# SiLU as one ScalarE instruction in the first scan of a scan-plus-attention kernel

## The chip, the core and the metric

The kernel runs on one core of a Trainium2 chip. The core has five engines that each take their instructions in order from a queue of their own and wait for each other through semaphores: TensorE (PE, with weight loads listed apart as PEld), VectorE (DVE), ScalarE (ACT), GpSimd (POOL) and SyncE (SP), which here only issues DMAs. The metric is the device time of one execution in microseconds (us), as the median of several runs. A lower time is better.

## The reference, cut to what matters

The input `x` has 32 sequences of 256 tokens with 256 channels. Two blocks follow each other: a gated state-space block with a recurrence over time, and two layers of local attention with a feed-forward part. The change touches only the first block:

```python
xr, gate = jnp.split(x @ W_in.T, 2, axis=-1)
xr = xr + t_emb[:, None, :]
xc = depthwise causal convolution of xr with 4 taps, + b_conv
xc = silu(xc)
xn = (xc - mean) / sqrt(var + 1e-5) * ln_g + ln_b
Bm, Cm, dt = split(xn @ W_xproj.T, 3)
dt = tanh(dt @ W_dt.T + b_dt) * 0.01
Ad = 1.0 - dt * tanh(A_log)
Bd = Bm * minimum(norm(xn), 1.0)
h  = clip(h * Ad + Bd * x_t, -10, 10)          # 256 steps, one after the other
y  = einsum(C_t, h) + D * xn
return (y * silu(gate)) @ W_out.T
```

`silu(v) = v * sigmoid(v)`, which is `0.5 * v * (1 + tanh(v / 2))`. The attention layers use `exp`, the feed-forward layers an exact `gelu`.

## The kernel before

**Tiling.** The 32 sequences are done in four groups of eight (`GB = 8`). In each group the recurrence walks through 256 steps in eight chunks of 32 (`CH = 32`); a step works on one tile of 128 partitions (16 states by 8 sequences) by 512 channels. While the attention and feed-forward layers of one group run, mainly on TensorE, the scan of the next group runs beside them. The first group's scan (`alone = g == 0`) has no layers beside it. TensorE uses that stretch to project the inputs of the three later groups ahead of time (`ahead_load`, `ahead_project`, `ahead_copy`, `ahead_put`).

**A chunk of the scan.** `project` multiplies the input by `W_in` into a PSUM bank, 128 channels at a time, so four of the eight projections feed the convolution and four the gate. `conv_in` (L471, L477) adds the condition on VectorE and starts the convolution on GpSimd; `conv_taps` (L488) adds three taps on VectorE. `conv_th` (L496) then puts `tanh(acc / 2)` into a tile `th` on ScalarE, and `conv_out` (L501) makes `(th + 1) * acc` on VectorE, which is twice the SiLU, in the tile `xc`. From `xc` TensorE makes the products `ps_raw` (L510) and the transpose `tp_x` (L540); VectorE takes its mean and variance (L550 to L554), ScalarE normalises (L569), GpSimd applies gain and offset (L576, L577), and SP writes the rows to DRAM as `xnd` (L581). The doubled SiLU changes nothing in the normalised value because the variance gets `4 * LN_EPS` in place of `LN_EPS`.

**A step.** SP loads row `t` of `xnd` into a tile `xrep`, repeated over the 16 states (`load_rows`, L675), from a pool of six buffers; in the first scan two rows in eight are spread by a matmul instead (`spread_rows`, L683). ScalarE scales the row by `beta` (`scale_row`, L696). VectorE then does the step itself, add and clip, as one custom instruction (`step`, L706) that needs the `h` of the step before. TensorE reads the output out of `h` (`read_out`, L718).

**The gate.** `gate_th` copies the gate's projection from PSUM into `sg` in the scan's order of tokens (`reorder`, L371, ScalarE) and puts its `tanh(sg / 2)` into `th_g` (L756, ScalarE). `gate_out` (L761) makes `(th_g + 1) * sg` on VectorE. `out_gate` (L787) multiplies it with the transposed scan output. The factor of two is taken out by `halve`, which multiplies `W_out` by 0.5 once. `project_y` (L796) and `copy_y` (L807) finish the block.

**Order of the work.** `at(slot, what)` writes an agenda by hand: conv work of a chunk 38 to 29 steps ahead of its first step, gate work 15 to 22 steps into the chunk. Tiles and waits come from pools; a scheduler in the recording layer then decides the order in which each engine's instructions stand, so removing an instruction can also move others. An order fixed by `tc.keep_in_program_order` is kept.

**ScalarE's tables.** ScalarE holds one set of activation functions at a time. The loads that change the set stand in the program as ACT_TABLE_LOAD; in the kernel before there is one at the start (L316), and then 123 ahead of `exp` (L1191) and 124 ahead of `gelu` (L1346), all of them after the first scan.

Of the kernel before, what the change touches and what calls it, by code (L numbers as in the profile page):

```python
# [13 lines left out]
AF = mybir.ActivationFunctionType  # L14
# [10 lines left out]
NC_ = DI // P  # L25
# [18 lines left out]
LN_EPS = 1e-5  # L44
# [29 lines left out]
def kernel(  # L74
# [29 lines left out]
    nc = tc.nc  # L104
# [58 lines left out]
    for j in range(NJ):  # L163
# [18 lines left out]
        out=mask_t[:, 0:W], in_=mask_t[:, 0:W], compare_op=ALU.is_ge, fill=MASKED_LOW,  # L182
# [3 lines left out]
        out=mask_t[:, W : 2 * W], in_=mask_t[:, W : 2 * W], compare_op=ALU.is_ge,  # L186
# [30 lines left out]
    for i in range(2):  # L217
        t = const.tile([P, NI * (P + GB)], FP, tag=f"ly{i}", name=f"ly{i}")
# [3 lines left out]
    def program(ctx, exact):  # L222
# [143 lines left out]
            for n in range(2 * L):  # L366
                at(50 + 6 * n, tables, n // L, n % L)

        def reorder(out, ps):

            nc.scalar.copy(  # L371
                out.rearrange("p (q i b) -> p b i q", q=NQ, b=GB),
                ps.rearrange("p (b i q) -> p b i q", q=NQ, b=GB),
            )

        def group_scan(g):
# [8 lines left out]
            alone = g == 0  # L385
# [3 lines left out]
            ck = [{} for _ in range(NCH)]  # L389

            def at(s, what, *args):
                agendas[-1].setdefault(s, []).append(partial(what, *args))
# [99 lines left out]

            def conv_th(c, ch):
                acc = ck[c]["xr", ch][1]
                th = sp.tile([P, GB * CH], FP, tag="th", name="th", bufs=2)
                nc.scalar.activation(th, acc.rearrange("p b t -> p (b t)"), AF.Tanh, scale=0.5)  # L496
                ck[c]["th", ch] = th
# [49 lines left out]
            def norm_stats(c, j):  # L547
                tp, stat = ck[c]["tp", j], ck[c]["stat"]
                st = sm.tile([P, 6], FP, tag="st", name="st")
                nc.vector.bn_stats(st, tp)  # L550
                mv = sm.tile([P, 2], FP, tag="mv", name="mv")
                nc.vector.bn_aggr(mv, st)
                ve = sm.tile([P, 1], FP, tag="ve", name="ve")
                nc.vector.tensor_scalar_add(ve, mv[:, 1:2], 4 * LN_EPS)  # L554
                nc.gpsimd.tensor_tensor(stat[:, j, 0:1], ve, neg_half[:, 0:1], ALU.pow)
                ck[c]["mv", j] = mv

# [192 lines left out]
            def gate_th(c, ch):  # L750
                if ch == 0:
                    ck[c]["sg"] = sp.tile([P, NC_, GB * CH], FP, tag="sg", name="sg")
                sg = ck[c]["sg"][:, ch]
                reorder(sg, ck[c].pop(("ps", NC_ + ch)))
                th = sp.tile([P, GB * CH], FP, tag="th", name="th_g", bufs=2)
                nc.scalar.activation(th, sg, AF.Tanh, scale=0.5)  # L756
                ck[c]["th_g", ch] = th
# [46 lines left out]

            def copy_y(c, d):
                yo = sp.tile([P, GB, CH], FP, tag="yo", name="yo", bufs=2)
                nc.scalar.copy(  # L807
                    yo.rearrange("p b (i q) -> p q i b", q=NQ),
                    ck[c].pop(("po", d))[:, 0 : GB * CH].rearrange(
                        "p (q i b) -> p q i b", q=NQ, b=GB  # L810
                    ),
                )
                ck[c]["yo", d] = yo

# [27 lines left out]
            for c in range(NCH):  # L842
                s0 = c * CH
                for hb in range(CH // TB):
                    s = s0 + hb * TB
                    for i in range(NI):
                        at(s + 4 * i + 5, read_out, c, hb, i)
                    at(s + 21, gated, c, hb)
                    at(s + 25, out_gate, c, hb)
                    at(s + 11, skip, c, hb)  # L850
                for ch in range(NC_):
                    at(s0 - 38 + 2 * ch, conv_in, c, ch)
                    at(s0 - 37 + 2 * ch, conv_taps, c, ch)
                    at(s0 - 36 + 2 * ch, conv_th, c, ch)
                    at(s0 - 35 + 2 * ch, conv_out, c, ch)
                for ch, s in enumerate((13, 16, 17, 18)):
                    at(s0 + s + 2, gate_th, c, ch)
                    at(s0 + s + 4, gate_out, c, ch)
                at(s0 - 25, raw_copy, c)
                at(s0 - 24, raw_turn, c)  # L860
                for j in range(NJ):
                    s = s0 - 26 + 4 * j
                    at(s + 2, norm_stats, c, j)
                    at(s + 4, norm_shift, c, j)
                    at(s + 5, norm_apply, c, j)
                    at(s + 6, norm_affine, c, j)
                    at(s + 9, norm_out, c, j)
                at(s0 - 11, length, c)
                at(s0 - 9, figures, c)
                at(s0 - 7, figures_in, c)  # L870
                at(s0 - 6, decay_th, c)
                at(s0 - 5, decays, c)
                at(s0 - 4, put_c, c, 0)
                at(s0 + 4, put_c, c, 1)
                for d in range(KM):
                    at(s0 + 45 + 2 * d, copy_y, c, d)
                    at(s0 + 46 + 2 * d, put_y, c, d)
            agendas.append({})
            for c in range(NCH):
                s0 = c * CH  # L880
# [19 lines left out]
                for hb in range(CH // TB):  # L900
                    s = s0 + hb * TB
# [5 lines left out]
            if alone:  # L907
                n = (NG - 1) * NCH * 2
                for u in range(n):
                    s = -30 + u * (NCH * CH) // n  # L910
# [6 lines left out]
        def scan_slots(groups):  # L917


            slots, scans = {}, [group_scan(g) for g in groups]  # L920
            for part in range(2):
                for i, agendas in enumerate(scans):
                    for s, what in agendas[part].items():
                        slots.setdefault(i * S + s, []).extend(what)
            for s in range(min(slots), max(slots) + 1):
                for what in slots.get(s, ()):
                    what()
                yield s
# [104 lines left out]
        if exact:  # L1033
# [4 lines left out]
                out=mask[:, 0:W], in_=mask[:, 0:W], compare_op=ALU.is_ge, fill=MASKED,  # L1038
# [3 lines left out]
                out=mask[:, W : 2 * W], in_=mask[:, W : 2 * W], compare_op=ALU.is_ge, fill=MASKED,  # L1042
# [448 lines left out]
        s0 = done[0]  # L1491
# [130 lines left out]
```

## Time and profile before

| what | value | from |
|---|---|---|
| median of three runs | 3637.98 us (3637.0 to 3640.93) | the times |
| time of the profiled execution | 3633.24 us | the times |
| its span | 3631.4 us | the page |
| PE, DVE, ACT, POOL busy, share of the span | 97%, 74%, 59%, 50% | the page, part 1 |
| first step of the first scan starts at | 56.92 us | the timeline of DVE |
| projection of the first attention layer starts at | 495.71 us | the chain |

The busy time of an engine is an average over stages with different limits: in the slices of the page TensorE reads 9 nearly throughout, while VectorE reads 8 or 9 in the first sixth and less later. Matmuls are pipelined and their ends are modelled, so a busy TensorE isn't TensorE at its peak. The profiled execution is 4.7 us faster than the median of the runs.

### The profile page before, as it was taken

What the parts mean: (1) busy time and instruction counts of PE and PEld (TensorE: products, weight loads), DVE (VectorE), ACT (ScalarE), POOL (GpSimd) and SP (SyncE); (2) the same over time, 40 slices, a digit from 0 to 9 for tenths busy, and PEclk for the clock granted to TensorE, in tenths of its full rate; (3) what the DMA queues carried; (4) which work ended last, traced back from release to release, by engine and by line L of the source; (5) the groups of instructions that cost most, each with busy time, mean ns of one, the idle gap of its engine ahead of it and who ended that gap; (6) DMA issues with size and microseconds to landing.
All of it is one profiled execution on the core that took longest, in us unless ns stands there. A gap on an engine that the chain in (4) does not pass through costs nothing.

```text
span 3631.4 us, 56312 instructions
## 1 busy us (share of the span) xinstructions
PE 3511.0 (97%) x19548; PEld 2271.0 (63%) x19548; DVE 2684.7 (74%) x5113; ACT 2160.2 (59%) x3689; POOL 1816.2 (50%) x1746
## 2 busy tenths in 40 slices
PE   7999989999999999999999999999999999999999
PEld 4444335666666666666666666666666677777677
DVE  5888889878887877877787878777877545555553
ACT  3566656666666666666666666666666444544443
POOL 4433456545555455545555556455544454544551
PEclk9999999999999999999999999999999999999999
DMA  7877665545554555444454555534454112011111
GB/s 196 210 203 207 184 174 144 133 114 135 133 138 127 148 143 145 132 118 123 117 141 125 134 150 138 139 105 129 114 140 119 52 44 66 12 30 33 37 27 37
DMA packets 468763, 435.59 MB, mean 120 GB/s; under 512 B 228724, under 2 KB 308085, under 8 KB 468341
## 3 DMA queue, kind: packets, MB, share of 16 engines
q1 hardware_dynamic: 384018, 419.88, 42.5%
q10 hardware_dynamic: 84450, 12.01, 2.1%
q8 instruction: 158, 2.59, 0.3%
q14 instruction: 137, 1.11, 0.1%
HBM read 383.54 MB, written 46.66 MB: 118 GB/s over the span
## 4 chain that ended last, share of the span: by engine, by line
PE 62%; DVE 18%; DMA 7%; POOL 6%; ACT 4%; issue 3%; SPq 0%; ACTq 0%; DVEq 0%; POOLq 0%
PE ps_qkv L973 13%; PE pa L1335 12%; DVE h L706 7%; PE po_f L1362 7%; PE y L718 4%; DMA xrep<-xnd 4%; PE ps_wo L1023 4%; PE sc L1182 4%; PE ov L1231 3%; DVE acc L488 2%; PE ps_out L796 2%; PE tr_qk L1012 2%; PE ps_in L398 2%; ACT xrep L696 2%; PE rs L1212 2%
## 5 line engine op out<-in xcount | busy, mean ns | idle before, releaser
L706 DVE CUSTOM_DVE_ANT_0 h<-h,xrep,lim 128x512 f32<-128x512 f32 x1024 | 950.8, 928 | 226.5 <-ACT xrep L696 193.6
L696 ACT ACTIVATE xrep<-xrep,beta 128x512 f32<-128x512 f32 x960 | 673.2, 719 | 356.6 <-DMA xrep<-xnd 258.0
L973 PE MATMUL ps_qkv<-qkv,res 128*128 128x512 f32 x1536 | 715.0, 600 | 21.0 <-DVE ag L1353 9.7
L1335 PE MATMUL pa<-hT,w 128*128 128x256 f32 (+1 forms) x2816 | 679.9, 383 | 1.6 <-ACT hT L1313 0.9
L1335 PEld LDWEIGHTS pa<-hT,w 128*128 128x128 f32 (+1 forms) x2816 | 514.9, 188 | 147.5 <-issue 55.7
L997 POOL TENSOR_TENSOR rot<-rot,swp 128x512 f32<-128x512 f32 x256 | 336.1, 1313 | 441.3 <-DVE swp L994 330.8
L973 PEld LDWEIGHTS ps_qkv<-qkv,res 128*128 128x128 f32 x1536 | 280.1, 190 | 310.4 <-issue 239.7
L1005 POOL TENSOR_TENSOR rn<-ss,neg_half 128x8 f32<-128x8 f32 x256 | 459.3, 1794 | 18.0 <-DVE ss L1003 8.0
L718 PE MATMUL y<-h,ly 128*32 128x512 f32 x2048 | 361.7, 615 | 11.7 <-DVE h L706 9.3
L1287 POOL TENSOR_TENSOR rstd<-ve,neg_half 128x2 f32<-128x2 f32 x64 | 46.3, 723 | 609.6 <-DVE ve L1285 592.1
L1362 PE MATMUL po_f<-ag,w 128*128 128x256 f32 x1280 | 307.4, 387 | 5.1 <-DVE fo L1373 5.1
L1006 POOL TENSOR_TENSOR rot<-rot,rn 128x512 f32<-128x512 f32 x256 | 292.4, 1142 | 20.1
L1353 DVE SCALAR_TENSOR_TENSOR ag<-pa,b_sb,ag 128x256 f32<-128x256 f32 x320 | 152.7, 477 | 197.7 <-ACT ag L1346 197.3
L1362 PEld LDWEIGHTS po_f<-ag,w 128*128 128x128 f32 x1280 | 236.1, 191 | 69.4 <-issue 11.9
L986 ACT ACTIVATE sq<-ps_qkv 128x512 f32<-128x512 f32 x256 | 151.8, 595 | 208.3 <-PE ps_qkv L973 148.7
L1346 ACT ACTIVATE ag<-pa,b_sb 128x256 f32<-128x256 f32 x320 | 150.1, 469 | 177.3 <-PE pa L1335 175.2
L488 DVE SCALAR_TENSOR_TENSOR acc<-xr,wc_sb,acc 128x256 f32<-128x256 f32 x384 | 192.5, 526 | 56.7 <-POOL acc L477 55.4
L1023 PE MATMUL ps_wo<-oT,wo 128*128 128x256 f32 x1024 | 231.7, 379 | 1.4 <-ACT ag L1346 1.4
L989 DVE TENSOR_TENSOR rot<-ps_qkv,rc_sb 128x512 f32<-128x512 f32 x256 | 175.3, 685 | 75.8 <-ACT sq L986 75.7
L1182 PE MATMUL sc<-qT,kT 64*128 64x128 f32 (+1 forms) x2048 | 219.6, 343 | 0.0
L1191 ACT ACTIVATE pT<-sc 128x512 f32<-128x512 f32 x384 | 208.4, 596 | 12.6 <-PE sc L1182 10.5
L1023 PEld LDWEIGHTS ps_wo<-oT,wo 128*128 128x128 f32 x1024 | 194.3, 190 | 29.3 <-ACT ag L1346 2.2
(157 smaller groups left out, 5653.3 us busy)
## 6 DMA issues: line engine op xcount, KB each, us to landing
xrep<-xnd SPq DMA_DIRECT2D x960, 256.0 KB
rb<-inv SPq DMA_DIRECT2D x128, 256.0 KB
xnd<-xn SPq DMA_DIRECT2D x64, 256.0 KB
qkv<-in_wqkv_dram SPq DMA_DIRECT2D x24, 512.0 KB
ahead<-xs_a SPq DMA_DIRECT2D x48, 256.0 KB
xp<-ahead SPq DMA_DIRECT2D x48, 256.0 KB
xd<-xnd SPq DMA_DIRECT2D x192, 64.0 KB
w<-in_w_dram SPq DMA_DIRECT2D x80, 128.0 KB
```

The source lines that it names most:

```text
L488: nc.vector.scalar_tensor_tensor(acc, xr[:, :, k : k + CH], wc_sb[:, ch, k : k + 1], acc, ALU.mult, ALU.add,)
L696: scaled = nc.scalar.activation(bx, ck[c].pop(("bx", t), bx), AF.Copy, scale=ck[c]["beta"][:, t : t + 1])
L706: nc.vector._custom_dve(TENSOR_ADD_SAT, out=h_new, in0=state["h"], in1=bx, s0=ck[c]["lim"][:, 0, t : t + 1], s1=ck[c]["lim"][:, 1, t : t + 1],
L718: nc.tensor.matmul(ck[c]["y", hb][32 * q : 32 * q + 32, :], ly[hb % 2][:, 32 * t : 32 * t + 32], ck[c].pop(("h", hb * TB + t)), start=(i = ...
L973: nc.tensor.matmul(ps, res[b][:, k, t0 : t0 + W], wt["qkv", a][:, k], start=(k == 0), stop=(k == KM - 1),)
L997: nc.gpsimd.tensor_add(rot, rot, swp)
L1005: nc.gpsimd.tensor_tensor(rn, ss, neg_half, ALU.pow)
L1006: nc.gpsimd.tensor_mul(rot, rot, bc(rn, 2, DH))
L1023: nc.tensor.matmul(po[:, d], wt["wo", 0][:, c, d * P : (d + 1) * P], oT[:, c, :], start=(c == 0), stop=(c == NC_ - 1),)
L1182: nc.tensor.matmul(banks[r][:, i, :], kT[rows, i0 + i, kw * W : (kw + 1) * W], qT[rows, i0 + i, kw * W :], start=self.apart, stop=self.apa ...
L1335: nc.tensor.matmul(dst[x], wt["w1", m][:, k, x], self.h[:, k], start=(k == 0), stop=(k == KM - 1),)
L1362: nc.tensor.matmul(self.po[:, d], wt["w2", 0][:, m, d * P : (d + 1) * P], self.ag[m], start=(m == 0), stop=(m == len(MCH) - 1),)
```

## The change

In the group that scans alone, ScalarE's SiLU takes the place of the tanh with VectorE's product, both in the convolution and in the gate. The convolution's SiLU is written to `xc` directly; the gate's is done by the instruction that reorders it out of PSUM. Both are then single, not doubled: the variance gets `LN_EPS` again, and the output copy multiplies by 2, since `W_out` stays halved for the later groups. Groups 1 to 3 compute as before; their copies in `reorder` and `copy_y` are now written as an activation with the function Copy.

```diff
-        def reorder(out, ps):
-            nc.scalar.copy(
+        def reorder(out, ps, func):
+            nc.scalar.activation(
                 out.rearrange("p (q i b) -> p b i q", q=NQ, b=GB),
                 ps.rearrange("p (b i q) -> p b i q", q=NQ, b=GB),
+                func,
             )
...
             def conv_th(c, ch):
                 acc = ck[c]["xr", ch][1]
+                if alone:
+                    ck[c].pop(("xr", ch))
+                    nc.scalar.activation(
+                        ck[c]["xc"][:, ch], acc.rearrange("p b t -> p (b t)"), AF.Silu
+                    )
+                    return
...
-                nc.vector.tensor_scalar_add(ve, mv[:, 1:2], 4 * LN_EPS)
+                nc.vector.tensor_scalar_add(
+                    ve, mv[:, 1:2], LN_EPS if alone else 4 * LN_EPS
+                )
...
                 sg = ck[c]["sg"][:, ch]
-                reorder(sg, ck[c].pop(("ps", NC_ + ch)))
+                reorder(sg, ck[c].pop(("ps", NC_ + ch)), AF.Silu if alone else AF.Copy)
+                if alone:
+                    return
...
-                nc.scalar.copy(
+                nc.scalar.activation(
                     yo.rearrange("p b (i q) -> p q i b", q=NQ),
                     ck[c].pop(("po", d))[:, 0 : GB * CH].rearrange(
                         "p (q i b) -> p q i b", q=NQ, b=GB
                     ),
+                    AF.Copy,
+                    scale=2.0 if alone else 1.0,
                 )
...
-                    at(s0 - 35 + 2 * ch, conv_out, c, ch)
+                    if not alone:
+                        at(s0 - 35 + 2 * ch, conv_out, c, ch)
...
-                    at(s0 + s + 4, gate_out, c, ch)
+                    if not alone:
+                        at(s0 + s + 4, gate_out, c, ch)
```

## The prediction

> **What bounds the kernel now.** I read the page first. Its busy line, and its slices for PE and DVE:
>
> ```profile
> PE 3511.0 (97%) x19548; PEld 2271.0 (63%) x19548; DVE 2684.7 (74%) x5113; ACT 2160.2 (59%) x3689; POOL 1816.2 (50%) x1746
> PE   7999989999999999999999999999999999999999
> DVE  5888889878887877877787878777877545555553
> ```
>
> TensorE bounds the whole, but the change acts only in the first five of the 40 slices (0 to about 490 us). So I cut the span there: before the first step, the first scan, the changeover to attention, the rest. Columns: stretch, length, busy time (instructions) of PE, PEld, DVE, ACT, POOL, then granted clock, DMA share, GB/s.
>
> ```profile
> 0.00:57.00 57.00, 36.26 (x154) 26.91 (x155) 25.38 (x75) 10.90 (x23) 24.78 (x69) 0.87 0.75 189
> 57.00:490.00 433.00, 403.32 (x1621) 191.66 (x1620) 374.23 (x692) 274.57 (x502) 175.58 (x217) 0.96 0.76 201
> 490.00:600.00 110.00, 93.58 (x471) 46.32 (x472) 96.72 (x170) 62.82 (x117) 76.30 (x68) 0.92 0.57 159
> 600.00:3631.00 3031.00, 2977.80 (x17308) 2006.09 (x17304) 2188.43 (x4180) 1811.88 (x3049) 1539.58 (x1392) 1.00 0.40 106
> ```
>
> From 600 us TensorE has 2977.8 of 3031 us, 98%. In the first scan it reads 93%, but that is elastic: read-out matmuls take about 1.0 us for eight records when they come together and 0.97 us for two that come alone (the timeline of PE at 349 to 392 us). VectorE has 374.2 of 433 us, 86%, and cannot be packed closer, because the steps follow each other. It is the bound here, so I asked what its idle 59 us wait for:
>
> ```profile
> DVE acc L488 <- POOL acc L477: 12.9, 23, 3.8
> DVE h L706 <- ACT xrep L696: 11.3, 15, 2.0
> DVE xc L501 <- ACT th L496: 8.7, 11, 1.7
> DVE st L550 <- PE tp_x L540: 7.2, 6, 1.4
> DVE ad L638 <- ACT ad L633: 4.8, 4, 1.9
> ```
>
> (Total us, times, longest.) Many short waits, no large one; 8.7 us are for the tanh that the change removes. The waits of ScalarE show the rival: 88.6 us for rows of `xrep` from DMA.
>
> **What the Trainium skill says.** The page "ScalarE activation tables: per-element evaluation and per-set limits", section "What a function is on this engine", says that the same operands cost the same whichever function is read, and that functions in one set need no switch. "ScalarE: Activation LUTs", section "What ACT_TABLE_LOAD costs", gives a load as 1283 ns plus a drain of 1380 ns. This trace agrees on the load (mean 1283 ns in every group) and doesn't show a drain as a piece of its own. No SiLU is in the trace, so the first statement is tested by the changed kernel.
>
> **The change part by part.** The rows concerned, from the groups of 0 to 700 us with shapes apart (busy us, mean ns, idle before):
>
> ```profile
> L371 ACT COPY sg<-ps_in 128x256 f32<-128x256 f32 x44 | 27.5, 635 | 1.5 <-PE ps_in L398 1.1 <-PE sc L1175 0.4
> L761 DVE SCALAR_TENSOR_TENSOR sg<-th_g,sg 128x256 f32<-128x256 f32 x44 | 22.5, 512 | 0.5 <-ACT th_g L756 0.5
> L501 DVE SCALAR_TENSOR_TENSOR xc<-th,acc 128x256 f32<-128x256 f32 x52 | 22.3, 434 | 13.9 <-ACT th L496 13.8
> L496 ACT ACTIVATE th<-acc 128x256 f32<-128x256 f32 x52 | 21.0, 412 | 35.4 <-DVE acc L488 20.1 <-DMA flg_sb<-in_f_ln_g_dram 7.0 <-DMA b_sb<-in_b_dram 3.8
> ```
>
> 1. VectorE loses 4 products of the convolution and 4 of the gate in each of 8 chunks, 64 in all. What one occupies is less than its duration, as instructions overlap; the timeline of DVE shows it:
>
> ```profile
> 189.23 0.42 DVE L761 SCALAR_TENSOR_TENSOR sg<-th_g,sg 128x256 f32<-128x256 f32 x1
> 189.56 0.81 DVE L706 CUSTOM_DVE_ANT_0 h<-h,xrep,lim 128x512 f32<-128x512 f32 x1
> 190.28 0.42 DVE L761 SCALAR_TENSOR_TENSOR sg<-th_g,sg 128x256 f32<-128x256 f32 x1
> 190.62 0.81 DVE L706 CUSTOM_DVE_ANT_0 h<-h,xrep,lim 128x512 f32<-128x512 f32 x1
> ```
>
> 189.23 to 189.56 and 190.28 to 190.62 are 0.34 us each; the products of `xc` show the same (207.20 less 206.86). Six of the 64 stand before the first step (6 records in 0 to 57 us), where VectorE is busy 25 of 57 us and the way goes over DMA and TensorE; I count them as nothing. If that cover were gone they would be worth 2 us. The other 58 by 0.34 give -19.7 us.
>
> 2. VectorE's 8.7 us wait for the tanh goes, but the SiLU stands in the same place on ScalarE, behind the same rows, and what is late next is the transpose `tp_x`: VectorE waits for it at L550. The instruction order of the changed kernel shows by how much this improves. Before, the last product of a chunk stood up to three steps behind in VectorE's row (after step 69) what ScalarE does ahead of the tanh (after row 72). Now the SiLU comes after row 71 and L550 after step 70: one row ahead instead of three, but TensorE's turn in between. I take half, -4.4 us, with 0 and -8.7 as ends.
>
> 3. `acc`'s buffer is freed by ScalarE and no longer by VectorE. GpSimd waits 25.6 us for that product over the whole run, and VectorE 12.9 us for GpSimd. Ends: 0 and half of 12.9, -6.5 us. I take 0, since GpSimd's start is also tied to `xr` and to its own queue.
>
> 4. ScalarE loses 32 tanhs of the gate, 13 us at 412 ns, over a scan in which it is busy 275 of 433 us. It doesn't bound there: nothing. The reordering with SiLU and the SiLU of `acc` I price like the copy (635 ns) and the tanh (412 ns) they replace. Were each 0.1 us longer, 64 would be 6 us on an engine with 158 us idle.
>
> 5. Two table loads come, as the order shows (250 in place of 248): one ahead of the first SiLU, near 17 us, one ahead of the first `exp` of attention. The tanh of the decays and the copies follow the SiLUs without a load between, so no load falls within the chunks. The first lies on the way to the first step: +1.3 us, ends 0 (ScalarE waits 3.8 us for a DMA soon after) and +2.7 with the page's drain. The second has ScalarE's idle time around it: 0 to 2.7, taken as 0.
>
> 6. Steps now follow each other closer, so rows can come late. There are six `xrep` buffers: a row is asked for when the step six before is done. Issue 0.52 us, landing 4.1 to 6.6 us (pieces of the chain), scaling 0.72, step 0.81: some 6.2 to 8.7 us for six steps, 1.0 to 1.4 us a step, where the mean is now 433 over 272 steps, 1.59. On average there is room, in dense stretches there isn't (17 steps from 176.8 to 200.4 us, 1.39 each, with waits of 0.7 us for `xrep`). I give back a fifth of the 19.7: +4 us, ends 0 and +16.
>
> 7. The variance's constant, the scale of 2 and the copies written as activations change no count and hardly a duration: nothing. TensorE's order is the same from the third twentieth of its row on; SP's moves weight loads by some chunks within the first scan, far ahead of their use: nothing.
>
> Sum: -19.7 - 4.4 + 1.3 + 4 = -18.8 us. Behind the first scan TensorE is bound and its order unchanged, so all of it should arrive at the end. Against the profiled execution: 3633.2 - 18.8 = 3614.4 us. The runs' median is 4.7 us above it; the same saving there gives 3619.2 us.
>
> **The rivals.**
>
> Rows bind (item 6 at +16): DMA runs at 76% in the first scan and ScalarE waits 88.6 us for rows; VectorE's freed time turns into waits for `xrep`. Then -19.7 - 4.4 + 1.3 + 16 = -6.8, 3631 us, no change that can be told. Against it: VectorE waits only 11.3 us for `xrep` today.
>
> More than the product goes: both upper ends of items 2 and 3 with nothing given back, -19.7 - 8.7 - 6.5 + 1.3 = -33.6, 3604 us. For it speaks the shorter chain; against it, that waits with several causes seldom vanish whole.
>
> Slower: the last SiLU of a chunk waits on ScalarE behind a row that hasn't landed, and L550 stops VectorE, and with it the row's own buffer cycle. ScalarE's longest wait for a row in the first scan is 4.3 us. At 4 us more in each of 7 chunks, 28 - 18.8 = +9, 3647 us. It decides from 18.8 / 7 = 2.7 us a chunk. Against it: the row in question was asked for five steps earlier, 5 us even at 1.0 us a step, and the same pair stood three rows apart before.
>
> The change doing nothing is excluded: the order shows 64 fewer VectorE instructions.
>
> **How the numbers follow.** This kernel's runs can tell about 0.2%, 7.3 us: below 3630.7 is faster, above 3645.3 slower. Forecast (-8 to -27): 0.66. Rows bind, near -7 or less: 0.17. More goes: 0.09. Slower: 0.08. Faster 0.66 + 0.09 + 0.02 of the rows' case = 0.77, same 0.15, slower 0.08. The range 3602 to 3634 leaves out the slower case, most of what is beyond -36 and part of the rows' case.
>
> **What would show it.** Step 1: L501 and L761 32 fewer each, the stretch from first to last step of the first scan about 20 us shorter, VectorE still near 86% in it. Step 2: L550's wait for `tp_x` above 7.2 us but less than 15.9. Step 4: SiLU at 0.4 us, in the reordering at 0.64. Step 5: one load near 17 us, one ahead of the first `exp` (at 529 us before). Step 6: VectorE's wait for `xrep` between 11 and 20 us. The prediction is wrong if the wait for `xrep` or `tp_x` grows by some 16 us, if a SiLU takes clearly longer than the tanh, or if TensorE's stretch after 600 us changes its length.

## The result, and the profile after

The changed kernel takes 3620.14 us (median of five runs, 3611.26 to 3625.62) where the kernel before took 3637.98 us. The ratio is 0.9949, with a 95% interval of 0.9933 to 0.9965, so it is 12 to 24 us faster. The forecast was 3619 us. A second measurement of the changed kernel, made with the first experiments, gave 3610.99 against 3633.68 us, a ratio of 0.9942 (0.9925 to 0.996).

The profiled execution took 3624.1 us (span 3622.3), only 9.1 us less than the profiled execution of before, while the medians differ by 17.8. Single executions scatter by that much: in the profiles of all kernels of this study the first step starts between 49.4 and 58.1 us, and from step 256 to the end they take 3166 to 3179 us. I therefore use medians of several runs for what an edit is worth, and profiles for where inside the scan it shows.

The busy line and the slices of PE and DVE on the page of the changed kernel:

```profile
PE 3510.2 (97%) x19548; PEld 2282.4 (63%) x19548; DVE 2666.1 (74%) x5049; ACT 2151.6 (59%) x3659; POOL 1801.9 (50%) x1746
PE   8999989999999999999999999999999999999999
DVE  5888889888787877887787778877777545555553
```

VectorE has 5049 instructions in place of 5113, the 64 products. ScalarE has 3659 in place of 3689: 32 tanhs less and two table loads more. The shares of the span haven't moved.

The stretch from the first step to step 256 of the first scan, with the columns of the prediction's windows (stretch, length, busy time and instructions of PE, PEld, DVE, ACT, POOL, granted clock, DMA share, GB/s). First the kernel before:

```profile
56.92:462.54 405.62, 376.63 (x1540) 181.95 (x1538) 351.11 (x649) 259.05 (x474) 164.66 (x201) 0.96 0.76 202
```

Then the kernel after, and its stretch from 600 us on:

```profile
56.93:447.77 390.84, 364.10 (x1538) 183.19 (x1536) 335.15 (x592) 246.28 (x442) 152.05 (x202) 0.97 0.81 211
600.00:3622.00 3022.00, 2968.82 (x17240) 2002.98 (x17234) 2176.59 (x4151) 1805.02 (x3035) 1534.77 (x1385) 1.00 0.40 105
```

In these two profiles the scans start at the same moment, and the second is 14.8 us shorter. VectorE is busy 16.0 us less and idle 55.7 us where it was 54.5. So by VectorE's own account the product's time has gone and nothing else has changed much. The experiments will show that this account, although it adds up, is not the main cause. From 600 us TensorE still has 98%.

The equal start is a coincidence of these two executions. The last of the first chunk's four `xc` is done at 24.8 us in the changed kernel and at 28.5 us before. Then TensorE, which makes the transposes and sums on the way to the first step, ran at a granted clock of 0.50 in the changed kernel's profile, at 0.71 in that of before and at 0.87 in the second profile of the changed kernel. The stretch from 25 to 37 us in these three, in this order:

```profile
25.00:37.00 12.00, 12.00 (x44) 10.03 (x44) 2.61 (x7) 2.45 (x5) 4.80 (x7) 0.50 0.51 163
25.00:37.00 12.00, 11.14 (x55) 8.62 (x56) 4.96 (x9) 1.86 (x4) 4.21 (x9) 0.71 0.58 178
25.00:37.00 12.00, 12.00 (x72) 9.77 (x71) 3.53 (x11) 3.77 (x8) 6.03 (x9) 0.87 0.63 193
```

In that second profile the first step starts at 50.77 us. In the two profiles of this study whose convolution keeps the tanh it starts at 56.9 and 58.1 us, in the eleven others with SiLU there at 49.4 to 55.0. So up to some 6 us of the gain may lie ahead of the first step. Two profiles against twelve, with different clocks, don't show it.

VectorE's waits from the first step to step 256 of the changed kernel (total us, times, longest):

```profile
DVE h L716 <- ACT xrep L706: 14.9, 22, 2.2
DVE ad L648 <- ACT ad L643: 10.4, 6, 3.0
DVE acc L489 <- POOL acc L478: 8.1, 22, 0.8
DVE st L558 <- PE tp_x L548: 6.0, 6, 1.2
DVE xc L509 <- ACT th L504: 3.1, 4, 1.0
```

In the same stretch of before they were 11.3 us for `xrep`, 4.8 for `ad`, 8.7 for `acc`, 7.2 for `tp_x` and 8.7 for the tanh; the 3.1 us left of that belong to the second group, whose convolution begins here. The wait that grew most is one that the prediction didn't name: `ad`, the decays, which VectorE (L648) multiplies once ScalarE has made their tanh (L643).

The groups of 0 to 700 us that answer to the rows of the prediction (busy us, mean ns, idle before):

```profile
L371 ACT ACTIVATE sg<-ps_in 128x256 f32<-128x256 f32 x44 | 28.5, 658 | 1.8 <-DMA rb<-inv 1.0 <-PE sc L1191 0.4 <-PE ps_in L399 0.3
L499 ACT ACTIVATE xc<-acc 128x256 f32<-128x256 f32 x32 | 13.1, 411 | 10.8 <-DVE acc L489 10.6
L509 DVE SCALAR_TENSOR_TENSOR xc<-th,acc 128x256 f32<-128x256 f32 x20 | 8.3, 430 | 5.5 <-ACT th L504 5.4
L499 ACT ACT_TABLE_LOAD x1 | 1.3, 1283 | 6.7 <-DMA w_out_sb<-in_w_outT_dram 6.7
```

The convolution's SiLU takes 411 ns, the tanh took 412. In the reordering the 32 SiLUs have a median of 664 ns, where the copies of the first scan had 626; that is 32 times 38 ns, 1.2 us. The load stands at 16.25 us and no other falls within the chunks. A load stands ahead of the first `exp` at 517 us.

### The profile page after: what moved, and what is told of

Read it like the earlier page. It is cut to its first block, busy times and chain, and to the rows that moved or that the text cites. A ratio compares the mean times of both kernels' runs of the same rounds, so it can differ in the third digit from the quotient of the medians.

```text
span 3622.3 us, 56212 instructions
## 1 busy us (share of the span) xinstructions
PE 3510.2 (97%) x19548; PEld 2282.4 (63%) x19548; DVE 2666.1 (74%) x5049; ACT 2151.6 (59%) x3659; POOL 1801.9 (50%) x1746
## 4 chain that ended last, share of the span: by engine, by line
PE 63%; DVE 16%; DMA 7%; POOL 6%; ACT 4%; issue 3%; SPq 1%; ACTq 0%; DVEq 0%; POOLq 0%
PE ps_qkv L989 13%; PE pa L1351 13%; PE po_f L1378 7%; DVE h L716 6%; DMA xrep<-xnd 5%; PE ps_wo L1039 4%; PE y L728 4%; PE sc L1198 4%; PE ov L1247 3%; PE ps_out L808 3%; PE tr_qk L1028 2%; DVE acc L489 2%; ACT xrep L706 2%; PE rs L1228 2%; PE ps_in L399 2%
## 5 line engine op out<-in xcount | busy, mean ns | idle before, releaser
L728 PE MATMUL y<-h,ly 128*32 128x512 f32 x2048 | 346.5, 611 | 12.5 <-DVE h L716 11.4
L1378 PE MATMUL po_f<-ag,w 128*128 128x256 f32 x1280 | 307.9, 388 | 4.9 <-DVE fo L1389 4.9
L1378 PEld LDWEIGHTS po_f<-ag,w 128*128 128x128 f32 x1280 | 236.5, 191 | 69.2 <-issue 12.8
L1198 PEld LDWEIGHTS sc<-qT,kT 64*128 64x128 f32 x2048 | 150.8, 187 | 99.8 <-issue 92.7
```

What stands on the lines that cost most here:

```text
L728: nc.tensor.matmul(ck[c]["y", hb][32 * q : 32 * q + 32, :], ly[hb % 2][:, 32 * t : 32 * t + 32], ck[c].pop(("h", hb * TB + t)), start=(i = ...
L1198: nc.tensor.matmul(banks[r][:, i, :], kT[rows, i0 + i, kw * W : (kw + 1) * W], qT[rows, i0 + i, kw * W :], start=self.apart, stop=self.apa ...
L1378: nc.tensor.matmul(self.po[:, d], wt["w2", 0][:, m, d * P : (d + 1) * P], self.ag[m], start=(m == 0), stop=(m == len(MCH) - 1),)
```

## The experiments

The expectations name their theories by letters. V is the prediction's own: VectorE bounds the first scan, so the 64 products make the gain and the 32 tanhs that leave ScalarE are worth nothing. S says that the shorter way from the convolution's taps to the transpose counts. When the first results fitted neither, V2 (half the products, half the wait for the tanh) and A (ScalarE's own time counts) followed. P says that ScalarE's time counts only where the gate's work meets the rows, and R that the supply of rows binds. Every kernel was timed beside the kernel before on the same chip. Since the chips differ from experiment to experiment, kernels are compared by their ratios to it.

One caution holds for all: the scheduler reorders instructions with every edit. Take the 205 instructions of ScalarE up to step 256 that are neither row scalings nor among those added or removed, and count the rows ahead of each. In the changed kernel 91 of them stand behind another number of rows than before. Where moved tanhs, loads or the first tap are added below, 3, 14 and 14 differ from the changed kernel; with the gate's half alone 26, with the products put back 39. With the convolution's half alone it is 83, with the tanhs put back in place 84, with both back 88, and these three are nearer to the order of before (34, 25 and 54). So among these kernels ScalarE's order comes in two families, and which of them a kernel gets goes with whether the gate's tanhs stand in place. An edit is therefore never only what its diff says.

### The changed kernel once more, and each half alone

The changed kernel was timed again, to share its chip with the halves.

> The changed kernel once more, beside the kernel before on the same chip. Theory V (VectorE's occupancy bounds the first scan, so that what is taken off its queue comes off the time): 14 to 23 us faster than before, ratio 0.994 to 0.996; steps 0 to 256 of the first scan some 15 to 19 us shorter. Theory S (what counted is the shorter way from the taps over ScalarE to the transpose; VectorE's freed time is lost in waits): the same total. This run only says how far one profile of the changed kernel differs from another.

The first half keeps the convolution's SiLU and puts the gate's tanh and product back (the output copy's factor is 1 again):

```diff
-                reorder(sg, ck[c].pop(("ps", NC_ + ch)), AF.Silu if alone else AF.Copy)
-                if alone:
-                    return
+                reorder(sg, ck[c].pop(("ps", NC_ + ch)), AF.Copy)
...
-                    if not alone:
-                        at(s0 + s + 4, gate_out, c, ch)
+                    at(s0 + s + 4, gate_out, c, ch)
```

> SiLU in the convolution alone; the gate keeps tanh and product. 32 VectorE instructions less, of which 26 lie behind the first step. Theory V: 26 x 0.34 = 8.8 us off steps 0 to 256, total 7 to 11 us faster than before. Theory S: nearly the whole gain is here, since only this part shortens the way from taps to transpose: 14 to 19 us faster than before.

The second keeps the gate's SiLU and puts the convolution's tanh and product back, with the variance's constant of before:

```diff
-                if alone:
-                    ck[c].pop(("xr", ch))
-                    nc.scalar.activation(
-                        ck[c]["xc"][:, ch], acc.rearrange("p b t -> p (b t)"), AF.Silu
-                    )
-                    return
...
-                    if not alone:
-                        at(s0 - 35 + 2 * ch, conv_out, c, ch)
+                    at(s0 - 35 + 2 * ch, conv_out, c, ch)
```

> SiLU in the gate alone; the convolution keeps tanh and product. 32 VectorE instructions and 32 ScalarE instructions less. Theory V: 32 x 0.34 = 10.9 us off the first scan, total 9 to 13 us faster than before. Theory S: the gate isn't on that way, 0 to 4 us faster.

Measured: the whole change 3610.99 us, the convolution alone 3625.66 (ratio 0.998, 0.997 to 0.9991), the gate alone 3625.82 (0.9981, 0.9972 to 0.999), against 3633.68. Each half is worth 8 us, together 16, and the whole 23 here and 18 in the first measurement, which the intervals don't tell from a sum. For the convolution V had expected 7 to 11 us and S 14 to 19, for the gate V 9 to 13 and S 0 to 4. The gate's half takes 32 tanhs off ScalarE and the convolution's takes none, yet they are worth the same; that settles nothing about the tanhs, since the halves also differ in the waits they remove. So the two kinds of work had to be put back one by one.

### Products put back, tanhs put back, both

Here the changed kernel computes its result as it is and does spare work beside it. The first adds 64 products on VectorE in the slots of the old ones. They read two constant tiles and nobody reads them, so they take VectorE's time, and no wait of theirs for a tanh shows in the traces:

```diff
+            def spare(c, ch):
+                th = sp.tile([P, GB * CH], FP, tag="th", name="spare", bufs=2)
+                nc.vector.scalar_tensor_tensor(
+                    th, lng_sb[:, 0 : GB * CH], 1.0, lnb_sb[:, 0 : GB * CH], ALU.add, ALU.mult
+                )
...
-                    if not alone:
-                        at(s0 - 35 + 2 * ch, conv_out, c, ch)
+                    at(s0 - 35 + 2 * ch, spare if alone else conv_out, c, ch)
...
-                    if not alone:
-                        at(s0 + s + 4, gate_out, c, ch)
+                    at(s0 + s + 4, spare if alone else gate_out, c, ch)
```

> The changed kernel with a spare product on VectorE in each of the 64 places where one was removed; it reads two constant tiles, its result is not used, and nothing waits for it. Theory V: the whole gain is gone, within 5 us of the time before. Theory S: the spare products only fill waits, 12 to 18 us faster than before, as the changed kernel.

The second adds the 32 tanhs of the gate on ScalarE, each behind its SiLU; in the first group nobody reads them:

```diff
                 reorder(sg, ck[c].pop(("ps", NC_ + ch)), AF.Silu if alone else AF.Copy)
-                if alone:
-                    return
                 th = sp.tile([P, GB * CH], FP, tag="th", name="th_g", bufs=2)
                 nc.scalar.activation(th, sg, AF.Tanh, scale=0.5)
-                ck[c]["th_g", ch] = th
+                if not alone:
+                    ck[c]["th_g", ch] = th
```

> The changed kernel with the gate's 32 tanhs put back on ScalarE; they read sg and write a scratch tile that nobody reads. Theory V2 (of the gain some 10 us are the products' own time on VectorE, the rest is that VectorE no longer stands waiting for a tanh; ScalarE's time is free): 17 to 23 us faster than before, as the changed kernel. Theory A (the rest is ScalarE's own 13 us, since it hands every row to VectorE): only 8 to 13 us faster than before.

The third has both edits at once.

> The changed kernel with the spare products on VectorE and the spare tanhs on ScalarE both back, none with a consumer. What is left of the change is that VectorE waits for no tanh, and that xc is ready one hand-over earlier. Theory V2: 9 to 14 us faster than before, as with the spare products alone. Theory A: within 4 us of the time before.

Measured, as ratio to the kernel before with its interval, and from the profile VectorE's busy and idle time from the first step to step 256:

| | tanhs on ScalarE | tanhs gone |
|---|---|---|
| products on VectorE | both back: 1.0 (0.9991 to 1.0008); 353.0 busy, 51.9 idle | products back: 0.9967 (0.9958 to 0.9977); 345.5 busy, 52.4 idle |
| products gone | tanhs back: 0.9989 (0.9981 to 0.9997); 330.6 busy, 75.5 idle | the change: 0.9949 and 0.9942; 335.2 busy, 55.7 idle |

The table reads both ways. Here "products" and "tanhs" are spare work, and the tanhs' presence includes the order of instructions that comes with them. Taking the tanhs away is worth 0.0033 of 3634 us, 12 us, with the products there, and 0.0040 to 0.0047, 15 to 17 us, without them. Taking the products away is worth 0.0011, 4 us, with the tanhs there, and 0.0018 to 0.0025, 7 to 9 us, without. By the intervals each difference is uncertain by some 4 to 7 us, so the tanhs' share is clear of it, the products' 7 to 9 us are at its edge, and their 4 us in the left column could be nothing. Most of the gain comes with taking ScalarE's tanhs out of their place. The theories fared unevenly: the products back gave 12 us, in S's range (12 to 18) and outside V's; the tanhs back 4 us, below the ranges of both V2 (17 to 23) and A (8 to 13); both back what A expected. The kernel with both back is no faster than before, although its spare products wait for no tanh: without the wait, but with all the work, nothing is gained. One tie is left in it: spare tanhs and spare products take turns in the two buffers of `th`, and ScalarE's tanhs wait 1.9 us for products.

The lower left is the instructive cell. There VectorE has lost the same products, its busy time has fallen by some 20 us against before, and its idle time has grown from 54.5 to 75.5 us: within this stretch all of it is given back. The stretch from the first step to step 256 of the kernel with the tanhs back, and VectorE's waits in it:

```profile
52.38:458.46 406.08, 377.73 (x1540) 181.33 (x1538) 330.56 (x593) 255.19 (x473) 158.63 (x203) 0.96 0.75 203
DVE ad L648 <- ACT ad L643: 14.3, 6, 3.9
DVE st L558 <- PE tp_x L548: 13.5, 12, 2.6
```

With both back, where `tp_x` shows what became of the wait for the tanh:

```profile
DVE st L564 <- PE tp_x L554: 13.8, 11, 2.0
DVE h L722 <- ACT xrep L712: 7.6, 11, 2.0
```

The 8.7 us for the tanh are gone there, and the wait for the transpose has grown from 7.2 to 13.8 us: the wait has moved by one instruction.

Where in a chunk does it happen? The gate's projections are copied and activated between steps 15 and 24 of a chunk (counted from 0, as the chunks are), where ScalarE also has the rows, the normalising and the copies. I cut that stretch out of chunks 1 to 7, by the starts of the steps, and summed the seven; the line gives length and busy time of the engines. Before:

```profile
sum 96.34, PE 74.36 PEld 40.95 DVE 85.25 ACT 84.36 POOL 41.01; mean PE 10.62 PEld 5.85 DVE 12.18 ACT 12.05 POOL 5.86
```

After:

```profile
sum 87.49, PE 80.73 PEld 46.07 DVE 74.65 ACT 71.00 POOL 38.82; mean PE 11.53 PEld 6.58 DVE 10.66 ACT 10.14 POOL 5.55
```

Both back, then the products back alone, then the tanhs back alone, each with the sum of the seven stretches between (from step 24 to step 15 of the next chunk) behind it:

```profile
sum 98.34, PE 77.29 PEld 42.90 DVE 88.66 ACT 85.97 POOL 43.09; mean PE 11.04 PEld 6.13 DVE 12.67 ACT 12.28 POOL 6.16
sum 260.53, PE 253.74 PEld 118.40 DVE 225.12 ACT 140.83 POOL 101.62; mean PE 36.25 PEld 16.91 DVE 32.16 ACT 20.12 POOL 14.52
```

```profile
sum 87.04, PE 76.30 PEld 43.42 DVE 80.74 ACT 74.89 POOL 43.75; mean PE 10.90 PEld 6.20 DVE 11.53 ACT 10.70 POOL 6.25
sum 263.39, PE 252.96 PEld 116.88 DVE 226.55 ACT 142.26 POOL 102.51; mean PE 36.14 PEld 16.70 DVE 32.36 ACT 20.32 POOL 14.64
```

```profile
sum 90.07, PE 76.37 PEld 42.13 DVE 73.20 ACT 81.17 POOL 38.78; mean PE 10.91 PEld 6.02 DVE 10.46 ACT 11.60 POOL 5.54
sum 266.73, PE 254.37 PEld 118.26 DVE 220.60 ACT 142.82 POOL 101.08; mean PE 36.34 PEld 16.89 DVE 31.51 ACT 20.40 POOL 14.44
```

Before, VectorE is busy 85.25 and ScalarE 84.36 of 96.34 us, 88% each. Over the scan ScalarE reads 64%; here it is as full as VectorE. With the products left in place, taking the tanhs away shortens the stretch from 98.34 to 87.04 us, 11.3 us, and the rest of the chunks grows by 2.9. Taking the products away shortens it from 98.34 to 90.07 us, 8.3 us, but there the rest grows by 6.2, with the waits for `ad` and `tp_x` shown above. So either removal relieves the dense stretch, and that of the tanhs keeps most of what it wins. With the products gone, however, taking the tanhs away shortens the stretch by only 2.6 us (90.07 to 87.49) and the rest by 8.2 (266.73 to 258.52). A full ScalarE in the dense stretch is therefore not shown to be the whole of the tanhs' price. Why the rest changes is not settled: the order of the caution above is one candidate.

### The same tanhs in another place, and loads in place of tanhs

The 32 spare tanhs are put into slots 24 to 27 of a chunk, where ScalarE is busy 46% of the time in the changed kernel, and not behind the SiLUs:

```diff
+            def spare_th(c, ch):
+                th = sp.tile([P, GB * CH], FP, tag="th", name="spare", bufs=2)
+                nc.scalar.activation(th, ck[c]["sg"][:, ch], AF.Tanh, scale=0.5)
...
                     at(s0 + s + 2, gate_th, c, ch)
+                    if alone:
+                        at(s0 + 24 + ch, spare_th, c, ch)
```

> The changed kernel with the 32 spare tanhs of the gate's size back on ScalarE, but 24 to 27 steps into the chunk, where ScalarE is busy 46% of the time, and not 15 to 20 steps into it, where it is busy 86 to 93%. Theory P (a ScalarE instruction costs its time only in the stretch of the gate, where rows, normalisation, copies and gate come together): 15 to 23 us faster than before, as the changed kernel. Theory A (ScalarE's time counts wherever it falls): 13 us are lost, 3 to 8 us faster than before.

The other adds an `exp` of one column behind the tanh of the decays in every chunk. Nobody reads it; it forces two table loads a chunk, 16 more than the 250 of the changed kernel, 20.5 us of ScalarE at 1283 ns each:

```diff
                 nc.scalar.activation(ad, ck[c]["bcd"][:, 2], AF.Tanh, bias=wbias[:, 2:3])
+                if alone:
+                    e = sm.tile([P, 1], FP, tag="e", name="e")
+                    nc.scalar.activation(e, ck[c]["bcd"][:, 2, 0:1], AF.Exp)
```

> The changed kernel with an exp of one column after the tanh of the decays in every chunk of the first scan, which nobody reads; it forces ScalarE to change its set to exp and back to SiLU in each chunk, 16 loads more (266 in place of 250). Theory V2: 16 x 1.28 = 20.5 us on an engine with some 145 us idle, so 0 to 8 us slower than the changed kernel, 10 to 22 us faster than before. Theory A: 16 to 24 us slower than the changed kernel, within 5 us of the time before.

Measured: the moved tanhs 3613.81 against 3634.92 us, a ratio of 0.9948 (0.9933 to 0.9964). That is the changed kernel's own ratio, and clear of the 0.9989 (0.9981 to 0.9997) that the same 32 tanhs gave in place. The extra loads gave 3616.34 against 3633.41, 0.9952 (0.9939 to 0.9965), so 20.5 us of loads cost 1 to 4 us by the ratios, within their intervals nothing. From the groups of the kernel with the moved tanhs, and its gate stretch:

```profile
L517 ACT ACTIVATE spare<-sg 128x256 f32<-128x256 f32 x32 | 12.7, 408 | 0.0
```

```profile
sum 83.19, PE 79.45 PEld 45.39 DVE 74.67 ACT 72.06 POOL 39.50; mean PE 11.35 PEld 6.48 DVE 10.67 ACT 10.29 POOL 5.64
```

In the trace these tanhs run in steps 21 to 27, mostly some five steps later than those in place, and 4.3 us of them still fall into the seven gate stretches, where it was 11.2 us with the tanhs in place. The same 12.7 us of work is on ScalarE, the gate stretch is short, and the gain is whole. So what these tanhs cost is decided by where they stand and not by how much work they are. Whether their place costs through the time they take there or through the order that the scheduler then makes, no kernel here can tell: the moved tanhs leave the order of the changed kernel, the tanhs in place don't, and none has the tanhs in place with the order of the changed kernel.

### The supply of rows

One buffer less for `xrep` in all groups (the opposite, more than six, wasn't tried):

```diff
-        xp = ctx.enter_context(tc.tile_pool(name="xp", bufs=6, reuse_waits="tile"))
+        xp = ctx.enter_context(tc.tile_pool(name="xp", bufs=5, reuse_waits="tile"))
```

> The changed kernel with five xrep buffers in place of six. It prices the supply of rows. Theory R (rows bind the first scan after the change, DMA and buffers): the cycle of a buffer, 6.2 to 8.7 us, is spread over five steps, up to a fifth longer in dense stretches: 15 us or more slower than the changed kernel, and later groups slower too. Theory P (the row is there when ScalarE comes to it, except at a few places): 0 to 8 us slower than the changed kernel.

Measured: 3635.13 against 3634.92 us, 1.0005 (0.9998 to 1.0012). VectorE's waits:

```profile
DVE h L716 <- ACT xrep L706: 39.7, 38, 2.5
```

With five buffers VectorE waits 39.7 us for rows, and all that the change gained is lost. Not all in the first scan: that takes 401.8 us to step 256, 11 more than in the changed kernel. From there to the end the profile takes 3178.5 us, 4 to 12 more than the two of the changed kernel; the later groups use the same pool. A loss of 15 us or more is what theory R expected. At six buffers the wait was 14.9 us, so rows were not the main limit there, but the margin is one buffer.

### Three attempts at a faster kernel

The wait for `ad` had grown, so its inputs and its tanh were moved one slot ahead:

```diff
+                e = 1 if alone else 0
...
-                at(s0 - 7, figures_in, c)
-                at(s0 - 6, decay_th, c)
...
+                at(s0 - 7 - e, figures_in, c)
+                at(s0 - 6 - e, decay_th, c)
```

> The changed kernel with the first scan's figures and the tanh of the decays one step earlier in the agenda, the VectorE work that needs that tanh where it was. In the changed kernel's profile VectorE waits about 10 us for it, 4.8 us before the change. If that wait is real and not replaced: 3 to 9 us faster than the changed kernel. If something else is late at the same place (the rows behind it): no difference.

`length`, `figures` and `figures_out` moved with them. Measured: 3617.92 against 3633.41 us, 0.9961 (0.9948 to 0.9975). The wait for `ad` fell from 10.4 to 1.4 us, that for `tp_x` rose from 6.0 to 10.8, and nothing was gained.

Next, the gate stretch was thinned: the last two of the gate's projections come two and three slots later, and the block's output projection and copies eight to eleven:

```diff
+            gates = (13, 16, 19, 21) if alone else (13, 16, 17, 18)
...
-                for ch, s in enumerate((13, 16, 17, 18)):
+                for ch, s in enumerate(gates):
...
+                e = 11 if alone and c < NCH - 1 else 0
...
-                    at(s0 + 45 + 2 * d, copy_y, c, d)
...
+                    at(s0 + 45 + e + 2 * d, copy_y, c, d)
...
-                    at(s0 + 43 + 2 * d, project_y, c, d)
+                    at(s0 + 43 + (8 if alone and c < NCH - 1 else 0) + 2 * d, project_y, c, d)
```

> The changed kernel with the stretch of the gate thinned out: the last two gate columns go to 21 and 23 steps into the chunk (19 and 20 before), the two output copies to 24 and 26 steps (13 and 15 before; the last chunk keeps its places). No instruction more or less. Theory P: some 2.5 us of ScalarE's work per chunk leave the dense stretch, a quarter to half of it counts: 5 to 10 us faster than the changed kernel. Theory A: no difference.

Measured: 3632.72 against 3634.92 us, 0.9999 (0.9988 to 1.001), so the whole gain was lost. VectorE's waits:

```profile
DVE h L716 <- ACT xrep L706: 21.5, 20, 3.3
DVE h L716 <- PE y L728: 9.8, 7, 3.3
```

The steps now wait 9.8 us until TensorE has read out an older `h`, a wait that hardly existed (0.3 us in the changed kernel), and longer for rows. By these waits the work had not become lighter, it had met TensorE's.

Last, the first tap of the convolution went from GpSimd to ScalarE, in the hope that VectorE, which waits 8.1 us for it, would wait less:

```diff
+                if alone:
+                    nc.scalar.activation(
+                        acc, xr[:, :, 0:CH], AF.Identity,
+                        bias=bconv_sb[:, ch : ch + 1], scale=wc_sb[:, ch, 0:1],
+                    )
+                else:
+                    nc.gpsimd.tensor_scalar(
...
```

> The changed kernel with the convolution's first tap in the first scan moved from GpSimd (about 1.04 us each) to ScalarE, 32 instructions of some 0.5 to 0.6 us, 28 to 33 steps ahead of their chunk's end, where ScalarE is busy 46 to 60%. VectorE waits 8 us for that tap in the changed kernel. Theory P (ScalarE's time outside the gate's stretch is free): the wait for the tap shrinks and 2 to 8 us more are gained, 18 to 29 us faster than before. Theory A (ScalarE's time counts wherever it falls): 17 us of ScalarE come on, 0 to 6 us faster than before.

Measured: 3620.02 against 3635.69 us, 0.9954 (0.9941 to 0.9968), no better than the change. From the groups:

```profile
L479 ACT ACTIVATE acc<-xr,bconv_sb,wc_sb 128x256 f32<-128x256 f32 x32 | 19.1, 596 | 13.4 <-DVE xr L472 9.5 <-DVE wdT L270 2.6 <-POOL ly L675 1.2
```

VectorE's wait for `acc` stayed, 8.7 us now for ScalarE and 4.3 for GpSimd, and that for `xrep` rose to 22.7. Again 19 us more of ScalarE's work cost at most some microseconds, though here GpSimd was relieved of the same 32 operations. No kernel tried was faster than the changed one by more than the measurements can tell.

## Why the prediction was right, and where it was not

The total was right: 18.8 us were forecast, 17.8 and 22.7 were measured. Its split was not, so that the total came out is in good part luck.

**Step 1, the products.** The counts and the occupation came true: 64 instructions fewer, the scan 14.8 us shorter to step 256 and 15.6 to step 272 where about 20 were expected, and VectorE at 86% in it (335.15 of 390.84). As a cause the step was too large. With the tanhs left on ScalarE the products were worth 4 us (ratio 0.9989), with the tanhs gone 7 to 9, not 19.7. The six products ahead of the first step were taken as nothing, 2 us at most; that stretch may have given more, as said with the result. "Cannot be packed closer" was true of VectorE's share, yet its waits were ready to take up what was freed.

**Step 4, the tanhs at nothing, is the step that failed.** With the order of instructions that comes with them they were worth 12 to 17 us. The prediction read "busy 275 of 433 us" as "doesn't bound there", an average over chunks that hold a dense stretch and slack ones. Cut at steps 15 and 24 of each chunk, the trace of before had the warning: 84.36 of 96.34 us. The two errors nearly cancel.

**Step 2, half of the wait for the tanh.** The SiLU stands a row ahead of where the tanh stood in two of the seven chunks whose convolution runs within the scan, and behind the same row in the other five, so the reading of one chunk didn't hold for all. The wait for `tp_x` fell from 7.2 to 6.0 us where more than 7.2 was expected; the wait for `ad` rose from 4.8 to 10.4, which was not foreseen. Where the products and tanhs were put back and only the wait left out, nothing was gained (ratio 1.0, 0.9991 to 1.0008).

**Step 3, `acc`.** VectorE's wait for GpSimd's part of it went from 8.7 to 8.1 us: nothing, as taken.

**Step 5, the loads.** Two more, where they were expected, and none within the chunks. Their own price wasn't isolated; 16 more in the chunks cost 1 to 4 us by the ratios. The end of +2.7, with a drain, didn't come: in the kernel with those loads ScalarE's gap ahead of a load has a median of 18 ns and the gap behind it 12 ns. The prices of the SiLU held: the statement of the Trainium skill, page "ScalarE activation tables: per-element evaluation and per-set limits", section "What a function is on this engine", that the same operands cost the same, agrees with 411 ns against 412. The reordering with SiLU, priced at 635 ns, took 664.

**Step 6, the rows.** VectorE's wait for `xrep` rose from 11.3 to 14.9 us, 3.6 where 4 was given back. ScalarE's own wait for rows from DMA rose from 87.0 to 100.6 us, about as much as the 12.8 us by which its busy time fell. The kernel with five buffers shows that the room was narrow.

**Step 7 and the rest of the kernel.** The lead at step 272 was 15.6 us and at the end of the same pair 9.1. TensorE waits 4.1 us for an `ag_rem` tile (L1378) in the stretch of 600 to 1100 us, 2.3 before, which could be 1.8 of the 6.5 lost. In the second profile of the changed kernel the way from step 256 to the end is 3166.4 us, shorter than before's 3168.9, so I take the loss for the scatter of single executions, and the medians bear that out. It is not shown.

**The rivals.** That rows bind at six buffers, and that the last SiLU holds up the chain, did not happen: ScalarE's longest wait for a row was 4.3 us, as before. That more than the product goes was true, but not by the mechanism named: it was the tanhs in their place. What stays open is how much of the tanhs' price is ScalarE's time in the dense stretch, and how much the order of rows that the scheduler builds around them.

## What to carry to other kernels

Before an engine's removed work is costed at nothing, cut the trace by the phase of the repeating pattern in which that work stands: an engine at 64% over a loop can be at 88% where the work is. A sum of removed busy time and changed waits can match the total and still name the wrong cause, so put each kind of removed work back as spare work that nobody reads, alone and together, and compare the order of instructions too. The same work moved by a few slots into a slack phase can cost nothing.

## What the runs showed of the hardware that was not expected

A step of the scan takes 0.81 us, but 50 of the 256 in the changed kernel take over 0.9 us, up to 1.85 (40 before; the steps' busy time went from 232.8 to 239.4 us). Of the 50, 45 overlap with a GpSimd operation that combines two tiles of 512 columns; of the 206 shorter ones 12 do. The timeline of the changed kernel, cut to 137.15 to 139.0 us (start, us, engine):

```profile
137.19 1.30 POOL L758 TENSOR_TENSOR xd<-xq,dskip_sb 128x512 f32<-128x512 f32 x1 [0.68 <-PE tz L785]
137.19 1.84 DVE L716 CUSTOM_DVE_ANT_0 h<-h,xrep,lim 128x512 f32<-128x512 f32 x1
```

Both start together, and the step takes 1.03 us longer than alone. The Trainium skill, page "SBUF — State Buffer", section "SBUF: two separate sides", says that GpSimd and a VectorE instruction with two inputs in SBUF take turns on a shared pair of ports and that the later one blocks; the trace agrees, and shows it sharply. Of the 45 steps 32 end 0.545 to 0.553 us after the GpSimd operation does, however long before that they had started; the other 13 overlap with two, and the second ends 1.13 to 1.14 us after the step. So the step doesn't take the full sum of 1.30 and 0.81 us: some 0.55 of its 0.81 us is left when it is let through. Busy time of VectorE thus holds waiting of this kind. An estimate from the figures above: 256 steps of 0.81 us are 207 us, so some 32 of the 239.4 us, and 25 of the 232.8 before, are waiting and not work.
